# A graph network's first table built in groups of six tiles, and the table of the other ends moved into the first edge stage

## The chip, the cores and the metric

The kernel runs on one core of one Trainium2 chip. A core has five engines that run their own instruction queues: TensorE (PE in the profile; PEld is its weight load), VectorE (DVE), ScalarE (ACT), GpSimd (POOL) and SyncE (SP), which here only issues DMA transfers. They wait for each other through semaphores. The metric is the device time of the whole program in microseconds (us); lower is better. Besides plain runs there is one profiled execution, from which the profile comes.

## The reference

Two layers of a graph network run on 6250 nodes with 128 features and 106250 edges, which come sorted by their target node `dst`. In what the change touches, only the first layer counts:

```python
h = jnp.maximum(_layernorm(x, axis=-1), 0.0)
...
xl = x @ Wl + bl        # here x is h
xr = x @ Wr + br
e = edge_attr @ We
m = xl[src] + xr[dst] + e
m = jax.nn.leaky_relu(m, NEG_SLOPE)
logits = m @ att
...                     # softmax over the edges of one dst
out = jax.ops.segment_sum(xl[src] * alpha[:, None], dst, num_segments=n)
```

The second layer forms a message from `x[src]` and `x[dst]` of every edge, sums the messages over `dst`, and mixes the sum with the node's own features.

## The kernel before

**Tables.** The nodes are 49 tiles of 128. Two tables are made from the normalised features and written to device memory: `xl_d`, whose rows (128 values and one more, h·Wl·att scaled) are gathered by `src`, and `xr_d`, the table of the other ends, whose rows are read in windows, since `dst` is sorted. The first stage ("table stage", lines 218 to 291) makes both. It goes through seven groups of seven tiles. For a group, VectorE takes the statistics of every tile (L237, L238), ScalarE and VectorE make the scale and shift (L240 to L242). For each tile, ScalarE then makes `h` (L248), TensorE transposes it into PSUM (`tp`, L251), VectorE or ScalarE by turns copies it out into `h_sb`, where it stands by feature and is kept (L253), TensorE multiplies it with both weights side by side, 257 columns (`mm`, L255), VectorE adds the bias of the first part and stores it as `tl` (L256), and ScalarE copies the second part as `tr` (L257). One write for `tl` and one for `tr` leave per group through SP's queue (L258, L259). `h`, `tp`, `mm`, `tl` and `tr` have two buffers each. After the first group, the list of source nodes, loaded as rows, is turned into columns by eight transposes (`columns`, L203 to L210, called at L263); the gathers take their indices from these. The stage also looks at the order of the edges and makes a flag (L270 to L291), which every engine reads in order to branch: `general()` is a way for all inputs, `fast()` the one that is run here.

**First edge stage.** `fast()` prepares small tables (L780 to L843: edge weights and indices as columns, masks) and then runs the loop of L1020 over 104 steps of 1024 edges. Step `s` loads its window of `xr_d` into `W`, and the row `dlb` of local target numbers (`load`, L851); GpSimd issues eight indirect gathers of 128 rows of `xl_d` each into a tile `gl` (`gather`, L195 to L198), of which there are ten buffers; VectorE compares `dlb` with the partition's number (`one_hot_t`, L863); TensorE multiplies this with `W` (`expand`, L867), which spreads the window's rows to the edges; VectorE adds the gathered rows (L1033), and logits follow. Seven steps later (`LAG`, L893) the gathered rows of step `u = s - 7` are weighted with the softmax's factors (L1049), summed by a matmul (L1063) and stored; then their `gl` buffer is free.

**Later stages.** The node stage (L1100 to L1171) makes two tables for the second layer, and the second edge stage (L1286) gathers from one of them in the same manner, with 832 more gathers. It is not touched by the change.

**What sets the order.** In the two edge loops the order of each engine's instructions is that of the program text. In the table stage and in the preparing part of `fast()` a scheduler orders each engine's instructions; every engine then works its own queue strictly in order, and one waiting instruction holds up all behind it. SP's queue is in order too, waits included. A DMA that is issued from SP or ScalarE also waits for an earlier one whose semaphore it uses again.

Of the kernel before, what the change touches and what calls it, by code (L numbers as in the profile page):

```python
# [27 lines left out]
TG = 7  # L28
NG = NT // TG
# [7 lines left out]
WIN = 126  # L37
PACE = 60
SLACK = 96
TN = 4  # L40
NGR = NT // TN
CH = TN * P
WL = D + 1
# [5 lines left out]
def kernel(  # L49
# [39 lines left out]
    x_sb = state.tile([P, NT, D], F32, name="x_sb")  # L89
    h_sb = state.tile([P, NT, D], F32, name="h_sb")  # L90
# [3 lines left out]
    for g in range(NG):  # L94
        n = TG if g < NG - 1 else TG - 1
        nc.sync.dma_start(
            x_sb[:, g * TG : g * TG + n, :],
            x[g * TG * P : (g * TG + n) * P, :].rearrange("(t p) f -> p t f", p=P),
        )
# [3 lines left out]
    ident = consts.tile([P, P], F32, name="ident")  # L103
# [96 lines left out]
    def node_rows(table, g, n=TG):  # L200
        return table[g * TG * P : (g * TG + n) * P].rearrange("(t p) ... -> p t ...", p=P)
# [13 lines left out]
    xl_d = dram.tile([NP, WL], F32, name="xl_d")  # L215
    xr_d = dram.tile([NP + P, D], F32, name="xr_d")
    flag = consts.tile([1, 1], I32, name="flag")
    with tc.tile_pool(name="pre", bufs=2) as pp, tc.tile_pool(name="pre1", bufs=1) as p1, tc.tile_pool(
# [14 lines left out]
        for g in range(NG):  # L233
            mv = pp.tile([P, TG, 2], F32, name="mv")
            for j in range(TG):
                st = pp.tile([P, 6], F32, name="st")
                V.bn_stats(st, x_sb[:, g * TG + j, :])  # L237
                V.bn_aggr(mv[:, j, :], st)  # L238
            rstd = pp.tile([P, 2, TG], F32, name="rstd0")
            S.activation(rstd[:, 0, :], mv[:, :, 1], AF.Sqrt, bias=eps)  # L240
            V.reciprocal(rstd[:, 0, :], rstd[:, 0, :])
            V.scalar_tensor_tensor(rstd[:, 1, :], mv[:, :, 0], -1.0, rstd[:, 0, :],  # L242
                                   op0=ALU.mult, op1=ALU.mult)
            tl = pp.tile([P, TG, WL], F32, name="tl")
            tr = pp.tile([P, TG, D], F32, name="tr")
            for j in range(TG):
                h = pp.tile([P, D], F32, name="h")
                S.activation(h, x_sb[:, g * TG + j, :], AF.Relu, bias=rstd[:, 1, j : j + 1],  # L248
                             scale=rstd[:, 0, j : j + 1])
                tp = ps_p.tile([P, P], F32, name="tp")  # L250
                T.transpose(tp, h, ident)  # L251
                hT = h_sb[:, g * TG + j, :]
                (S.copy if j % 2 else V.tensor_copy)(hT, tp)  # L253
                mm = ps_p.tile([P, 2 * D + 1], F32, name="mm")
                T.matmul(mm, hT, w0c, start=True, stop=True)  # L255
                V.tensor_tensor(tl[:, j, :], mm[:, :WL], b0c, ALU.add)  # L256
                S.copy(tr[:, j, :], mm[:, WL:])  # L257
            nc.sync.dma_start(node_rows(xl_d, g), tl)  # L258
# [482 lines left out]
    def fast():  # L741
# [43 lines left out]
        with tc.tile_pool(name="col1", bufs=1) as p1, tc.tile_pool(name="rows", bufs=2) as rp, tc.tile_pool(  # L785
            name="ps_p", bufs=2, space=PSUM
        ) as ps_p:
# [6 lines left out]
            nc.sync.dma_start(dl_d, dl_b)  # L794

# [589 lines left out]
```

## Time and profile before

| | us |
|---|---|
| median of 3 runs | 3032.93 (3027.8 to 3052.9) |
| profiled execution, its own time | 2414.23 |
| its span, first to last instruction | 2412.4 |
| POOL busy in the span | 1699.7 (70%) |
| DVE busy | 1637.3 (68%) |
| PE busy | 1375.8 (57%) |
| ACT busy | 1276.6 (53%) |

The profiled execution is 619 us shorter than the median of the plain runs; the profile says nothing of where the plain runs spend these. In the span, the table stage takes the first 65 us, gathers from `xl_d` run from 71.6 us to about 1147 us, the node stage lies about 1150 to 1235 us, and the second edge stage fills nearly all of the rest.

A line of the costliest groups has the source line, the engine, the operation, what it writes and reads, and a count; then busy time and mean ns of one, and the idle time of the engine just before it with what ended that. A line of an answer in order of time has start and duration in us, engine, line and operation, and in brackets the idle time before it. A line of waits has who waited for whom, the sum in us, how often, and the longest one. The chain that ended last follows the work back from the last instruction to whatever released it.

### The profile page before, as it was taken

The numbers are of one execution on the slowest core, as the hardware profiler recorded it, in microseconds if no ns is written. First come the engines' busy times: TensorE is split into PE (matmuls) and PEld (weight loads), VectorE is DVE, ScalarE is ACT, GpSimd is POOL, SyncE is SP. The second block draws the span as 40 slices with busy tenths as digits, with TensorE's granted clock in tenths as the row PEclk, the third lists the DMA queues.
The fourth block names the chain that finished last, engine by engine and source line by source line (L and its number), as shares of the span: only waits on it lengthen the run. The fifth ranks groups of instructions, "written<-read, shape, count | busy, mean of one in ns | idle before, by whom it ended". The sixth has DMA issues, their size and how long they took to land.

```text
span 2412.4 us, 30614 instructions
## 1 busy us (share of the span) xinstructions
PE 1375.8 (57%) x7692; PEld 1270.8 (53%) x7692; DVE 1637.3 (68%) x3597; ACT 1276.6 (53%) x4267; POOL 1699.7 (70%) x1703
## 2 busy tenths in 40 slices
PE   6446555556566556565484555555655655555553
PEld 3345555555555455565464555555555654555553
DVE  6666677677677667767445567677767768768765
ACT  5223343334344334344456676676676677667663
POOL 1677777777777777777057777777777777777770
PEclk9667887787878777777687677778777777777876
DMA  6743455443443433443142333343333333333331
GB/s 166 211 114 92 111 151 137 98 100 92 101 100 92 98 96 92 100 100 80 32 132 79 90 94 99 85 107 97 83 107 97 85 108 103 83 101 102 85 96 30
DMA packets 217496, 242.90 MB, mean 101 GB/s; under 512 B 41373, under 2 KB 158077, under 8 KB 217309
## 3 DMA queue, kind: packets, MB, share of 16 engines
q0 software_dynamic: 53792, 110.57, 19.7%
q1 hardware_dynamic: 160657, 130.00, 18.5%
q8 instruction: 64, 1.05, 0.2%
q14 instruction: 123, 1.01, 0.1%
q10 hardware_dynamic: 2860, 0.27, 0.1%
HBM read 197.43 MB, written 43.25 MB: 100 GB/s over the span
## 4 chain that ended last, share of the span: by engine, by line
POOL 44%; issue 18%; DMA 14%; DVE 13%; PE 7%; ACT 3%; SPq 0%; DVEq 0%; another core or an unknown queue 0%; ACTq 0%; POOLq 0%
POOL gl L196 44%; DMA gl<-xl_d,src_c 7%; DMA gl<-a_d,src_c 5%; DVE y L1314 2%; DVE m_ps L1033 2%; PE agg_ps L1063 2%; DVE y L1298 1%; DVE oh L1309 1%; PE agg_ps L1329 1%; DVE y L1316 1%; PE mm L255 1%; PE mm L1156 1%; ACT sq L1303 1%; DVE oh L1040 1%; DVE oht L863 1%
## 5 line engine op out<-in xcount | busy, mean ns | idle before, releaser
L196 POOL DMA_INDIRECT gl<-xl_d,src_c x832 | 820.9, 987 | 308.8 <-issue 229.8
L196 POOL DMA_INDIRECT gl<-a_d,src_c x832 | 845.2, 1016 | 260.7 <-issue 234.3
L1329 PE MATMUL agg_ps<-glw,oh 128*128 128x129 f32 x1664 | 363.9, 403 | 485.7 <-ACT glw L1320 439.7
L1329 PEld LDWEIGHTS agg_ps<-glw,oh 128*128 128x128 f32 x1664 | 336.3, 298 | 505.8 <-ACT glw L1320 505.8
L1063 PE MATMUL agg_ps<-glw,oh 128*128 128x130 f32 x1664 | 345.0, 389 | 386.3 <-DVE glw L1043 206.8
L1063 PEld LDWEIGHTS agg_ps<-glw,oh 128*128 128x128 f32 x1664 | 320.7, 288 | 404.1 <-ACT glw L1049 404.1
L1034 ACT ACTIVATE m_ps<-m_ps 128x1024 f32<-128x1024 f32 x104 | 104.8, 1008 | 573.6 <-DVE m_ps L1033 429.3
L1303 ACT ACTIVATE sq<-y 128x128 f32<-128x128 f32 x832 | 257.1, 309 | 275.8 <-DVE y L1298 252.4
L1033 DVE TENSOR_TENSOR m_ps<-m_ps,gl 128x1024 f32<-128x1024 f32 x104 | 128.1, 1232 | 299.9 <-DMA gl<-xl_d,src_c 273.7
L867 PE MATMUL m_ps<-W,oht 128*128 128x128 f32 x1664 | 259.8, 320 | 36.2 <-DVE oht L863 22.8
L867 PEld LDWEIGHTS m_ps<-W,oht 128*128 128x128 f32 x1664 | 243.8, 233 | 45.2 <-issue 22.3
L1320 ACT ACTIVATE glw<-y,ew_c 128x128 f32<-128x128 f32 x832 | 254.4, 389 | 3.4
L1049 ACT ACTIVATE glw<-gl,exm 128x128 f32<-128x128 f32 x832 | 254.3, 394 | 0.0
L1298 DVE TENSOR_TENSOR y<-y_ps,gl 128x1024 f32<-128x1024 f32 x104 | 126.8, 1220 | 187.8 <-DMA gl<-a_d,src_c 146.7
L867 PE MATMUL y_ps<-W,oht 128*128 128x128 f32 x1664 | 230.4, 298 | 13.2 <-DVE oht L863 9.0
L867 PEld LDWEIGHTS y_ps<-W,oht 128*128 128x128 f32 x1664 | 226.7, 218 | 13.8 <-issue 13.8
L1314 DVE SCALAR_TENSOR_TENSOR y<-y,rs,mg_r 128x128 f32<-128x128 f32 x832 | 227.3, 344 | 0.0
L863 DVE TENSOR_SCALAR oht<-dlb,iota_p 126x1024 f32<-126x1024 bf16 x208 | 159.3, 766 | 15.1 <-DMA dlb<-dl_d 15.0
L1303 ACT ACTIVATION_READ_ACCUMULATOR sq<-y 128x1 f32 x832 | 155.0, 186 | 0.0
L1051 DVE TENSOR_TENSOR m_ps<-m_ps,att 128x1024 f32<-128x1024 f32 x104 | 131.3, 1263 | 4.8 <-ACT m_ps L1034 4.6
L1317 ACT ACTIVATE y<-y 128x1024 f32<-128x1024 f32 x104 | 109.9, 1057 | 41.1 <-DVE y L1316 41.0
L1316 DVE TENSOR_TENSOR y<-y,mb_r 128x1024 f32<-128x1024 f32 x104 | 127.7, 1228 | 3.6
(251 smaller groups left out, 1610.7 us busy)
## 6 DMA issues: line engine op xcount, KB each, us to landing
dlb<-dl_d SPq DMA_DIRECT2D x208, 256.0 KB
gl<-xl_d,src_c POOLq DMA_INDIRECT x832
gl<-a_d,src_c POOLq DMA_INDIRECT x832
res<-agg SPq DMA_DIRECT2D x104, 64.0 KB
res<-agg SPq DMA_DIRECT2D x104, 63.5 KB
W<-xr_d SPq DMA_DIRECT2D x104, 63.0 KB
W<-b_d SPq DMA_DIRECT2D x104, 63.0 KB
res<-zt SPq DMA_DIRECT2D x20, 325.0 KB
```

Source lines behind the costliest of these rows:

```text
L196: GP.indirect_dma_start(out=dest, out_offset=None, in_=table, in_offset=bass.IndirectOffsetOnAxis(ap=idx, axis=0))
L863: V.tensor_scalar(oht[:WIN, :], dlb[:WIN, :], iota_p[:WIN, :], None, op0=ALU.is_equal)
L867: T.matmul(ps[:, j, :], oht[:, j * P : (j + 1) * P], w, start=True, stop=True)
L1033: V.tensor_tensor(ps, ps, gl[:, :, :D], ALU.add)
L1049: S.activation(glw[:, j, :D], glu[:, j, :D], AF.Copy, scale=exm[b][:, q, j, 1:2])
L1063: T.matmul(aggs[u], oh[:, j, :], glw[:, j, :], start=(j == 0), stop=(j == ST - 1))
L1298: V.tensor_tensor(y, pss.pop(s), gl, ALU.add)
L1303: S.activation(sq, y[:, j, :], AF.Square, accum_out=rs[:, j : j + 1])
L1314: V.scalar_tensor_tensor(yu[:, j, :], yu[:, j, :], ru[:, j : j + 1], mg_r, op0=ALU.mult, op1=ALU.mult)
L1316: V.tensor_tensor(yu, yu, over_tiles(mb_r, ST), ALU.add)
L1320: S.activation(glw[:, j, :D], yu[:, j, :], AF.Copy, scale=ew_c[:, u, j : j + 1])
L1329: T.matmul(aggs[u], oh[:, j, :], glw[:, j, :], start=(j == 0), stop=(j == ST - 1))
```

## The change

The table stage now goes through groups of six tiles (the last has one). Three tiles share a PSUM tile: three transposes are followed by one copy of 384 columns, always on ScalarE, and three matmuls of 129 columns by one addition of the bias on VectorE. The weight tile holds only the first table's columns. The source list is turned into columns at the fourth group rather than the first, and `x` is loaded in eight groups of six tiles. The table of the other ends is no longer made here: in `fast()`, behind the write of the local target numbers, 13 groups of four tiles are multiplied straight from the kept `h_sb` with `Wr`, copied out of PSUM by ScalarE into one of two `tr` buffers, and written to `xr_d` on SP's queue, all ahead of the first load of a window.

```diff
+PG = 6
+PB = 3
...
-    for g in range(NG):
-        n = TG if g < NG - 1 else TG - 1
+    for g in range(NT // PG):
         nc.sync.dma_start(
-            x_sb[:, g * TG : g * TG + n, :],
-            x[g * TG * P : (g * TG + n) * P, :].rearrange("(t p) f -> p t f", p=P),
+            x_sb[:, g * PG : (g + 1) * PG, :],
+            x[g * PG * P : (g + 1) * PG * P, :].rearrange("(t p) f -> p t f", p=P),
         )
...
-        w0c = p1.tile([P, 2 * D + 1], F32, name="w0c")
+        w0c = p1.tile([P, WL], F32, name="w0c")
         b0c = p1.tile([P, WL], F32, name="b0c")
-        V.tensor_copy(w0c[:, WL:], w0[:, D:])
...
-        for g in range(NG):
-            mv = pp.tile([P, TG, 2], F32, name="mv")
-            for j in range(TG):
+        for t0 in range(0, NT, PG):
+            n = min(PG, NT - t0)
+            mv = pp.tile([P, PG, 2], F32, name="mv")
+            for j in range(n):
...
-            tl = pp.tile([P, TG, WL], F32, name="tl")
-            tr = pp.tile([P, TG, D], F32, name="tr")
-            for j in range(TG):
-                h = pp.tile([P, D], F32, name="h")
-                S.activation(h, x_sb[:, g * TG + j, :], AF.Relu, bias=rstd[:, 1, j : j + 1],
-                             scale=rstd[:, 0, j : j + 1])
-                tp = ps_p.tile([P, P], F32, name="tp")
-                T.transpose(tp, h, ident)
-                hT = h_sb[:, g * TG + j, :]
-                (S.copy if j % 2 else V.tensor_copy)(hT, tp)
-                mm = ps_p.tile([P, 2 * D + 1], F32, name="mm")
-                T.matmul(mm, hT, w0c, start=True, stop=True)
-                V.tensor_tensor(tl[:, j, :], mm[:, :WL], b0c, ALU.add)
-                S.copy(tr[:, j, :], mm[:, WL:])
-            nc.sync.dma_start(node_rows(xl_d, g), tl)
-            nc.sync.dma_start(node_rows(xr_d, g), tr)
-            if g == 0:
+            tl = pp.tile([P, PG, WL], F32, name="tl")
+            for q in range(0, n, PB):
+                k = min(PB, n - q)
+                tp = ps_p.tile([P, PB, P], F32, name="tp")
+                for j in range(q, q + k):
+                    h = pp.tile([P, D], F32, name="h")
+                    S.activation(h, x_sb[:, t0 + j, :], AF.Relu, bias=rstd[:, 1, j : j + 1],
+                                 scale=rstd[:, 0, j : j + 1])
+                    T.transpose(tp[:, j - q, :], h, ident)
+                S.copy(h_sb[:, t0 + q : t0 + q + k, :], tp[:, :k, :])
+                mm = ps_p.tile([P, PB, WL], F32, name="mm")
+                for j in range(k):
+                    T.matmul(mm[:, j, :], h_sb[:, t0 + q + j, :], w0c, start=True, stop=True)
+                V.tensor_tensor(tl[:, q : q + k, :], mm[:, :k, :],
+                                b0c[:, None, :].to_broadcast([P, k, WL]), ALU.add)
+            nc.sync.dma_start(xl_d[t0 * P : (t0 + n) * P].rearrange("(t p) f -> p t f", p=P), tl[:, :n, :])
+            if t0 == 3 * PG:
                 sr = p1.tile([NS, SE], F32, name="sr")
                 V.tensor_copy(sr, src_r)
                 columns(ps_k, src_c, sr, "ctp")
...
             nc.sync.dma_start(dl_d, dl_b)
+
+            for t0 in range(0, NT, TN):
+                n = min(TN, NT - t0)
+                rp_ = ps_x.tile([P, TN, D], F32, name="xr_ps")
+                for j in range(n):
+                    T.matmul(rp_[:, j, :], h_sb[:, t0 + j, :], w0[:, D:], start=True, stop=True)
+                tr = xp.tile([P, TN, D], F32, name="tr")
+                S.copy(tr[:, :n, :], rp_[:, :n, :])
+                nc.sync.dma_start(xr_d[t0 * P : (t0 + n) * P].rearrange("(t p) f -> p t f", p=P), tr[:, :n, :])
 
             for w in Ws:
```

More of the change, by code (lines that the diff above doesn't have):

```diff
@@ L232 @@
             V.tensor_scalar(o[:, D : D + 1], o[:, D : D + 1], 0.2, None, op0=ALU.mult)
-        for g in range(NG):
-            mv = pp.tile([P, TG, 2], F32, name="mv")
-            for j in range(TG):
+        for t0 in range(0, NT, PG):
+            n = min(PG, NT - t0)
+            mv = pp.tile([P, PG, 2], F32, name="mv")
+            for j in range(n):
                 st = pp.tile([P, 6], F32, name="st")
-                V.bn_stats(st, x_sb[:, g * TG + j, :])
+                V.bn_stats(st, x_sb[:, t0 + j, :])
@@ L238 @@
                 V.bn_aggr(mv[:, j, :], st)
[L239 to L242, printed above, removed]
+            rstd = pp.tile([P, 2, PG], F32, name="rstd0")
+            S.activation(rstd[:, 0, :n], mv[:, :n, 1], AF.Sqrt, bias=eps)
+            V.reciprocal(rstd[:, 0, :n], rstd[:, 0, :n])
@@ L243 @@
+            V.scalar_tensor_tensor(rstd[:, 1, :n], mv[:, :n, 0], -1.0, rstd[:, 0, :n],
                                    op0=ALU.mult, op1=ALU.mult)
-            tl = pp.tile([P, TG, WL], F32, name="tl")
-            tr = pp.tile([P, TG, D], F32, name="tr")
-            for j in range(TG):
-                h = pp.tile([P, D], F32, name="h")
-                S.activation(h, x_sb[:, g * TG + j, :], AF.Relu, bias=rstd[:, 1, j : j + 1],
-                             scale=rstd[:, 0, j : j + 1])
-                tp = ps_p.tile([P, P], F32, name="tp")
-                T.transpose(tp, h, ident)
-                hT = h_sb[:, g * TG + j, :]
-                (S.copy if j % 2 else V.tensor_copy)(hT, tp)
-                mm = ps_p.tile([P, 2 * D + 1], F32, name="mm")
-                T.matmul(mm, hT, w0c, start=True, stop=True)
-                V.tensor_tensor(tl[:, j, :], mm[:, :WL], b0c, ALU.add)
-                S.copy(tr[:, j, :], mm[:, WL:])
@@ L785, in fast @@
         with tc.tile_pool(name="col1", bufs=1) as p1, tc.tile_pool(name="rows", bufs=2) as rp, tc.tile_pool(
-            name="ps_p", bufs=2, space=PSUM
-        ) as ps_p:
+            name="xr", bufs=2
+        ) as xp, tc.tile_pool(name="ps_p", bufs=2, space=PSUM) as ps_p, tc.tile_pool(
+            name="ps_x", bufs=2, space=PSUM
+        ) as ps_x:
             base_f = p1.tile([NS, 1], F32, name="base_f")
```

## The prediction

> **What bounds the kernel now.** I read the chain of work that ended last, then the costliest groups, then GpSimd's waits, then the first 72 us in order of time. The page first:
>
> ```profile
> span 2412.4 us, 30614 instructions
> ...
> POOL 44%; issue 18%; DMA 14%; DVE 13%; PE 7%; ACT 3%; SPq 0%; DVEq 0%; another core or an unknown queue 0%; ACTq 0%; POOLq 0%
> ...
> L196 POOL DMA_INDIRECT gl<-xl_d,src_c x832 | 820.9, 987 | 308.8 <-issue 229.8
> ```
>
> GpSimd's gathers carry the chain. In the first edge stage there are 832, each 0.987 us plus idle before it; without one long wait that is (820.9 + 308.8 - 55.6)/832 = 1.291 us, so 10.33 us for a step of eight. GpSimd's waits up to 1260 us, where the second edge stage begins:
>
> ```profile
> POOL gl L196 <- issue: 230.4, 756, 0.3
> POOL x_sb L1134 <- PE ctr L1126: 80.4, 12, 63.9
> POOL gl L196 <- DMA W<-in_L_gnn_br_dram: 55.6, 1, 55.6
> POOL gl L196 <- DMA gl<-xl_d,src_c: 10.1, 33, 0.3
> ```
>
> No gather waits over 0.3 us for a buffer or a consumer; the one long wait, 55.6 us, is that of the first gather for the first table. So **the time of the first gather is worth its full length**: all that follows hangs on it. The end of the table stage in order of time:
>
> ```profile
> 65.06 0.29 DVE L256 TENSOR_TENSOR tl<-mm,b0c 128x129 f32<-128x129 f32 x1 [0.25 <-PE mm L255]
> 65.39 0.36 SPq L258 DMA_DIRECT2D xl_d<-tl  x1
> ...
> 69.59 0.60 DVE L780 MEMSET zt<- 128x650 f32 x1 [4.23 <-issue]
> ...
> 71.57 1.26 POOL L196 DMA_INDIRECT gl<-xl_d,src_c  x1 [55.55 <-DMA W<-in_L_gnn_br_dram]
> ```
>
> The last eviction ends at 65.35, its write of seven tiles lands 5.23 us after its issue (the chain's piece, 65.39 to 70.62), and the gather starts 0.95 later. The releaser named on the gather is only the latest event; the chain itself goes through the write. The stage's groups, up to 71 us:
>
> ```profile
> L255 PE MATMUL mm<-w0c,h_sb 128*128 128x257 f32 x98 | 33.5, 449 | 1.3 <-DVE h_sb L253 0.7 <-DVE mv L238 0.3
> L248 ACT ACTIVATE h<-x_sb,rstd 128x128 f32<-128x128 f32 x49 | 23.5, 495 | 4.5 <-PE tp L251 2.3 <-DMA x_sb<-in_x_dram 2.1
> ```
>
> From 30.0 to 65.4 TensorE is busy 33.3 of 35.4 us, ScalarE 30.1, VectorE 28.4 (busy time by stretch): TensorE is nearly full, ScalarE 85%. Before that everything stood from about 24 to 29.2 us for the source indices, whose load took 11.46 us.
>
> **What the Trainium skill says.** "PSUM — Partial Sum Buffer", The four PSUM rules: one matmul output stays in one 2 KiB bank. Three tiles of 129 words are 1548 B and fit, four would not; no run shows a limit here. "ScalarE: Activation LUTs", What ACT_TABLE_LOAD costs: 186 ns + 0.833 ns per element, 93 ns more for each pointer operand; h would be 479 ns, the trace has 495, it agrees. "DMA: Bandwidth & Descriptors", Anatomy of one DMA: about 2 us of a transfer are fixed; a gather's landing here is 2.44 us, which agrees. "Runtime: NRT & Kernel Launch", Instruction fetch mechanics: a taken branch can force a fetch; VectorE's 4.23 us above agree.
>
> **The change, part by part.**
> *Removed from the table stage.* The matmul has 129 columns in place of 257. Its two passes run at 0.33 us each in close bursts (six in 1.98); the 128-column m_ps matmul runs 0.128 a pass (sixteen in 2.05), so 2 x 0.33 falls to 2 x 0.13 = 0.26 us: 0.4 us a tile off TensorE. Gone are 49 copies tr (0.262 us, ScalarE) and seven xr_d writes.
> *Batched.* Three transposes, one ScalarE copy of 384: between the 128 copy (0.263) and the 512 one (0.586) that is 0.48 us. One VectorE add of 387: between 0.291 (129) and 1.232 (1024) that is 0.56 us.
> *What is left after the stall.* The order of the changed program has 15 tiles transposed before the source columns (before: 9), with 12 multiplied (before: 6). The index load is the same and queues behind the same 3.2 MB of x, so I keep 29.2 us and start at 30.0; that the columns moved to the fourth group gains six tiles of cover, but no earlier index. Then ScalarE has 33 h x 0.495 = 16.3, 11.3 copies x 0.48 = 5.4, two column copies 1.8, five roots 1.5: 25.1 us. TensorE: 34 transposes x 0.28 + 37 x 0.26 to 0.32 + 1.8 = 21 to 23. VectorE: 22 tiles x 0.44 statistics + 13 adds x 0.56 + about 7 for flags and reciprocals = 24. **ScalarE becomes the longest, with the others close.** At the old stretch of 35.4/30.1 = 1.18 it takes 29.6, unstretched 25.1; I take 27.4. The last three tiles' matmul and add: 1.0. The last write is now one tile, behind one of six: between 2.4 (a gather) and 5.2, I take 3.8, plus 0.95. First gather at 30.0 + 27.4 + 1.0 + 3.8 + 0.95 = 63.2 against 71.57: -8.4. Ends: 59.5 (-12.1) and 66.8 (-4.8). The new x groups (eight loads in place of seven) and the weight copy L227 (0.23) come before the stall and cost nothing as long as 29.2 stands.
> *Moved into the edge stage.* 49 matmuls (2 x 0.128 = 0.26: 12.5 us TensorE), 13 copies of 512 (0.586: 7.6 us ScalarE), 13 writes on SP. TensorE and ScalarE stand there anyway: up to 94.8 and 100.2 us they do little but column transposes. On SP the writes stand ahead of the loads of W, dlb and edge weights of step 0, and W reads xr_d, so it waits for all 13. The index and weight loads lie between them. On ScalarE the later copies hold up its queued column loads and the column copies; VectorE waits for the end-of-row loads. tr has two buffers: a pair costs a copy 0.59 + issue 0.41 + landing 3.8 = 4.8, and 6.5 pairs take 31 us. The last eviction is at 58.4 by the sum above, the branch takes the 4.23 us that it took before: 62.6. Then come 1.5 to begin, the 31, and 8.3 as before from the first dlb load (90.64) to the first add of gathered rows (98.94): the first add at 103.4, which is 40 us after the first gather (before: 27). **The cover:** ten gl buffers. Step 10's gathers start 103 us after the first; they need gl of step 0, freed in round 7, that is 7 x 5.8 (98.94 to 104.73) + 4 after the first add. So the add may come 58.7 us after the first gather; 18 us of slack remain, and the cost is nothing. Without that cover every microsecond of the 40 would be on the path.
> *Contention.* xr_d's 3.2 MB now run beside the first gathers, where 71 to 160 us already moves 182 GB/s. I take 1 us, from 0 to 4.
> *Sum:* -8.4 + 1 = -7.4 us on the profiled time of 2414.23 (span 2412.4 + 1.8 around it). The three timed runs' median is 3032.93, 619 us above it; the profile doesn't show where these lie. If they are spread evenly everything counts 1.256 times (-9.3), if they lie elsewhere once. I take -8: **3025**. With the ends, (-12.1) x 1.256 = -15 and -0.8.
>
> **The rivals.** Three runs of the kernel before differ by 25 us (3027.8 to 3052.9), so about 1%, 30 us, is what a measurement can tell from no change.
> *The stage doesn't shorten.* h keeps two buffers: a copy ends, three matmuls take 0.9 with their wait, the next transpose 0.27, then 0.2, one h 0.5, the copy 0.48, about 2.6 in all with waits: 0.87 us a tile, against 0.86 before (35.4/41). For: TensorE works in order, its transposes stand behind the matmuls, and ScalarE then idles between an h and the next though it has the most to do. Against: the order that was drawn up varies along the stage, in places four transposes run ahead of a matmul. With 34 tiles x 0.87 = 29.6, 1.8 for the column copies, 1.0, 3.8 and 0.95 the first gather is at 67.1, and 2 us later where VectorE's flag work (7 us) falls into that chain: -2 to -4, less 1 of contention; I take 3031.
> *Slower: the table of other ends comes too late.* Mechanism: two tr buffers, 13 writes in a row ahead of W. It decides from a landing of 6.6 us ((58.7 + 0.6 - 9.8)/6.5 - 1.0). Speaking for it: src_r took 11.46 under load. At that landing the pairs take 6.5 x 12.46 = 81, the first add is 32 us past the slack, net +24: 3057; at 14 us the pairs take 97.5, net +40: 3073; at 9 us they take 65, net +8: 3041. I take 3060. Against: the writes are small (256 KB), xl_d's of 452 KB landed in 5.23.
> *The hidden 619 us lie in the front.* If the unprofiled start is much longer than 71 us, a shorter one gains more: a gain of 40 in place of 8, 2993. Nothing in the profile speaks for it, nothing excludes it.
>
> **How the numbers follow.** Forecast 0.60 (3025); stage doesn't shorten 0.15 (3031); too late 0.10 (3060); front longer 0.15 (2993). The first two are within 1%; of the third half lies over +1% (landings past 12.5 us), half below. Faster by over 1% 0.15, within 1% 0.80, slower 0.05. The range takes the ends of the sum, 3033 - 15 and 3033 - 0.8, and half the runs' spread (12.5) on either side: 3005 to 3045. It leaves out the last rival (0.15) and the worse half of the third (0.05), and holds the rest.
>
> **What would show it.** Right: the first gather between 59 and 67 us, the gathers still 1.29 us apart, no wait over a microsecond on gl after it, span about 2405. ScalarE, not TensorE, fullest from 30 us on. Batching wrong: first gather later than 68. Lateness: a wait of GpSimd for ScalarE's glw near the eleventh step. Source stall wrong: the cast of the indices not near 29 us. The whole is wrong if the unprofiled time moves by more than 30 us while the span doesn't.

## The result and the profile after

| | us |
|---|---|
| before, median of 20 runs | 3033.97 (3022.09 to 3052.9) |
| after, median of 20 runs | 3065.35 (3033.55 to 3080.96) |
| after / before | 1.0085, 95% interval 1.0059 to 1.011 |
| after, the profiled execution's own time | 3073.72 (span 3071.9) |

The changed kernel is slower by 0.85%, 31 us between the medians. 3025 was forecast, with 3005 to 3045 as the range.

The kernel before runs at one of two levels, near 2414 us or near 3030 us (2990 us in one set), and keeps to one for a whole set of runs made beside each other on one chip; its first profile is of the short level, its timed runs above are of the long one.

The page of the changed kernel, to be set against the first fence of the prediction:

```profile
span 3071.9 us, 30732 instructions
...
DVE 25%; another core or an unknown queue 24%; ACT 22%; PE 13%; issue 11%; DMA 3%; POOL 1%; DVEq 0%; SPq 0%; ACTq 0%; POOLq 0%
...
L197 POOL DMA_INDIRECT gl<-xl_d,src_c x832 | 817.1, 982 | 660.8 <-ACT glw L1061 345.2
L197 POOL DMA_INDIRECT gl<-a_d,src_c x832 | 817.2, 982 | 541.9 <-DVE y L1310 286.6
```

GpSimd's gathers carried 44% of the chain before and carry 1% now; they wait for ScalarE's glw and VectorE's y. These are the gathered rows weighted with the softmax's factors in the first edge stage, and what the second one makes of its gathered rows; a gl buffer is free only when they are made. Most of this is not the change, though. A second profile of the kernel before, `before_again`, is of the long level (3034.98 us). GpSimd's waits there, and then those of the changed kernel from 60 to 300 us (who waited for whom, sum in us, times, longest):

```profile
POOL gl L196 <- issue: 467.3, 1485, 8.1
POOL gl L196 <- ACT glw L1049: 325.2, 43, 48.7
POOL gl L196 <- DVE y L1298: 279.3, 54, 12.0
```

```profile
POOL gl L197 <- ACT glw L1061: 73.1, 1, 73.1
POOL gl L197 <- DMA W<-in_L_gnn_We_dram: 51.9, 1, 51.9
POOL gl L197 <- issue: 43.2, 114, 8.8
```

The two waits of before are 604.5 us in all. The first profile had neither, and its span was 620.8 us shorter: this is where the "hidden 619 us" lie, spread over both edge stages. What the change adds is in the one long wait near the eleventh step: 73.1 in place of 48.7 us.

The front of three profiled executions, from their answers in order of time (the 81st gather is the first one that needs a freed gl buffer):

| us | before, short level | before, long level | after, long level |
|---|---|---|---|
| first gather | 71.57 | 71.24 | 68.79 |
| first add of gathered rows | 98.94 | 145.36 | 199.57 |
| 81st gather | 176.96 | 222.62 | 245.65 |

Against the long level, the first gather comes 2.5 us earlier and the 81st 23.0 us later. The two executions are 38.7 us apart (3034.98 and 3073.72, the latter 8 us above its kernel's median): 23.0 us lie up to the 81st gather, 15.7 behind it. From the 81st gather to the end of the span four executions of set 1 below took 2801 to 2816 us and this one 2826, so the 15.7 us can't be told from the scatter of single executions.

**The preparing part, after.** ScalarE and then VectorE in order of time (start, duration, engine, line; in brackets the idle time before and what ended it; `remote` is a releaser that the profile doesn't name, `issue` none that it shows):

```profile
98.08 0.90 ACT L211 COPY dl_c<-ctp 128x416 f32<-128x416 f32 x1 [4.30 <-PE ctp L209]
...
118.69 0.90 ACT L211 COPY dl_c<-ctp 128x416 f32<-128x416 f32 x1 [19.53 <-issue]
129.89 0.90 ACT L211 COPY fst_c<-ctp 128x416 f32<-128x416 f32 x1 [10.30 <-issue]
141.09 0.90 ACT L211 COPY fst_c<-ctp 128x416 f32<-128x416 f32 x1 [10.30 <-issue]
141.78 1.12 ACT L805 COPY tr<-xr_ps 128x512 f32<-128x512 f32 x2
182.41 0.90 ACT L211 COPY ew_c<-ctp 128x416 f32<-128x416 f32 x1 [39.51 <-remote]
```

```profile
194.95 0.75 DVE L875 TENSOR_SCALAR oht<-dlb,iota_p 126x1024 f32<-126x1024 bf16 x1 [46.22 <-DMA W<-xr_d]
...
199.57 1.23 DVE L1045 TENSOR_TENSOR m_ps<-m_ps,gl 128x1024 f32<-128x1024 f32 x1 [1.99 <-PE m_ps L879]
```

VectorE's first one-hot tile and first addition in the kernel before at the long level:

```profile
106.58 0.98 DVE L863 TENSOR_SCALAR oht<-dlb,iota_p 126x1024 f32<-126x1024 bf16 x1 [12.78 <-issue]
...
145.36 1.23 DVE L1033 TENSOR_TENSOR m_ps<-m_ps,gl 128x1024 f32<-128x1024 f32 x1 [30.94 <-remote]
```

In the changed kernel, GpSimd issues the 80 gathers of the ten gl buffers from 68.8 to 172 us, one behind the other. Up to 98 us the others work; then copies that take a microsecond stand 10 to 40 us apart. The work picks up about 10 us after the last of the 80 gathers (171.61), and only then is the table of other ends finished.

The same is seen in the loop of the kernel before at the long level. TensorE, VectorE and some of GpSimd's gathers:

```profile
614.77 0.20 PE L926 MATMUL tx<-ident,crow 1*32 1x1 f32 x2
...
622.80 0.94 POOL L196 DMA_INDIRECT gl<-xl_d,src_c  x1 [0.30 <-issue]
624.05 0.94 POOL L196 DMA_INDIRECT gl<-xl_d,src_c  x1 [0.30 <-issue]
627.53 0.15 DVE L929 COPY cc<-tx 32x2 f32<-32x2 f32 x1 [7.39 <-remote]
```

The copy at 627.53 needs the two transposes that ended at 614.97. It comes 12.6 us later, 2.5 us after the end of the last gather of a series, though VectorE had stood for 7.39 us. A lower granted TensorE clock (its mean is 0.688 here, 0.764 in the first profile) can't be the reason: the transposes were long done.

**The table stage, after.** Where the prediction counted on 8.4 us, there are 2.5 to 2.8. TensorE alone in stretches of 6 us (stretch, length, busy time and count, granted clock, DMA share, GB/s), before at the long level and then after:

```profile
36.00:42.00 6.00, 5.92 (x26) 1.00 0.63 160
48.00:54.00 6.00, 5.99 (x25) 1.00 0.57 150
54.00:60.00 6.00, 5.54 (x26) 1.00 0.62 161
```

```profile
36.00:42.00 6.00, 4.87 (x28) 0.92 0.44 125
48.00:54.00 6.00, 5.26 (x22) 0.50 0.18 53
54.00:60.00 6.00, 5.26 (x21) 0.50 0.27 79
```

From about 41 us on the batched stage runs at half the granted TensorE clock. The additions to tl, three tiles each, are then 2.82 us apart:

```profile
57.03 0.56 DVE L258 TENSOR_TENSOR tl<-mm,b0c 128x387 f32<-128x387 f32 x1 [1.99 <-PE mm L257]
...
59.85 0.56 DVE L258 TENSOR_TENSOR tl<-mm,b0c 128x387 f32<-128x387 f32 x1 [2.26 <-PE mm L257]
```

In an execution with the same stage whose clock was still 1.00 (`tr13`, below) they are 1.99 us apart:

```profile
51.00 0.56 DVE L258 TENSOR_TENSOR tl<-mm,b0c 128x387 f32<-128x387 f32 x1 [1.17 <-PE mm L257]
52.99 0.56 DVE L258 TENSOR_TENSOR tl<-mm,b0c 128x387 f32<-128x387 f32 x1 [1.43 <-PE mm L257]
```

### The profile page after: what moved, and what is told of

Its sections match the earlier page's. It is cut to its first block, busy times and chain, and to the rows that moved or that the text cites. A ratio compares the mean times of both kernels' runs of the same rounds, so it can differ in the third digit from the quotient of the medians.

```text
span 3071.9 us, 30732 instructions
## 1 busy us (share of the span) xinstructions
PE 1490.3 (49%) x7790; PEld 1338.4 (44%) x7790; DVE 1618.3 (53%) x3540; ACT 1282.7 (42%) x4229; POOL 1667.6 (54%) x1703
## 4 chain that ended last, share of the span: by engine, by line
DVE 25%; another core or an unknown queue 24%; ACT 22%; PE 13%; issue 11%; DMA 3%; POOL 1%; DVEq 0%; SPq 0%; ACTq 0%; POOLq 0%
ACT sq L1315 9%; PE agg_ps L1341 6%; ACT glw L1332 6%; DVE m_ps L1045 3%; DVE lr L1065 3%; ACT y L1329 3%; DVE m_ps L1063 3%; DVE oh L1052 3%; DVE y L1310 2%; DVE y L1326 2%; ACT glw L1061 2%; POOL gl L197 1%; PE agg_ps L1075 1%; DVE oh L1321 1%
## 5 line engine op out<-in xcount | busy, mean ns | idle before, releaser
L197 POOL DMA_INDIRECT gl<-a_d,src_c x832 | 817.2, 982 | 541.9 <-DVE y L1310 286.6
L1341 PE MATMUL agg_ps<-glw,oh 128*128 128x129 f32 x1664 | 433.6, 435 | 663.2 <-ACT glw L1332 491.3
L1075 PE MATMUL agg_ps<-glw,oh 128*128 128x130 f32 x1664 | 315.7, 364 | 532.3 <-ACT glw L1061 320.0
L879 PE MATMUL m_ps<-W,oht 128*128 128x128 f32 x1664 | 277.9, 322 | 160.9 <-issue 134.9
L879 PEld LDWEIGHTS m_ps<-W,oht 128*128 128x128 f32 x1664 | 250.8, 231 | 182.9 <-issue 152.8
L879 PE MATMUL y_ps<-W,oht 128*128 128x128 f32 x1664 | 267.8, 328 | 32.8 <-issue 23.8
L879 PEld LDWEIGHTS y_ps<-W,oht 128*128 128x128 f32 x1664 | 265.0, 249 | 33.1 <-issue 33.1
L1065 DVE TENSOR_REDUCE lr<-m_ps 128x8 f32<-128x1024 f32 x104 | 127.4, 1225 | 3.6
```

Of the source, the lines that this page charges most:

```text
L197: GP.indirect_dma_start(out=dest, out_offset=None, in_=table, in_offset=bass.IndirectOffsetOnAxis(ap=idx, axis=0))
L879: T.matmul(ps[:, j, :], oht[:, j * P : (j + 1) * P], w, start=True, stop=True)
L1065: V.tensor_reduce(lr, ps, AX.X, ALU.add)
L1075: T.matmul(aggs[u], oh[:, j, :], glw[:, j, :], start=(j == 0), stop=(j == ST - 1))
L1341: T.matmul(aggs[u], oh[:, j, :], glw[:, j, :], start=(j == 0), stop=(j == ST - 1))
```

## The experiments

The theory after the result: at the long level the other engines fall behind while gathers follow each other closely; the change puts more work (13 groups of matmul, copy and write, and W behind all of them) into the stretch where this happens, and so the ten gl buffers, which the prediction took for cover, are what holds the work up. Rivals: the batched stage itself costs the time; the writes ahead of W do, whatever the gathers; time is a plain sum of gathers and other work, which no placing of gathers changes. Runs came in six sets, each with its own runs of the kernel before: medians 3031.45, 2989.76, 2414.87, 2413.74, 3031.75 and 3037.2 us. Ratios are against the set's own; intervals are 95%.

### Before once more (set 1)

No edit.

> The kernel before, looked at once more, because its first profiled execution took 2414 us and its timed runs 3033. If the front loss of the changed kernel is new, the first add of gathered rows comes about 27 us after the first gather here too, and no wait of GpSimd for ScalarE's glw near the eleventh step exceeds 1 us. If an execution of some 3033 us always has the other engines standing while gathers run one behind the other, its span is near 3030 us, the first add comes 80 to 110 us after the first gather, and GpSimd has a wait of 20 to 50 us for glw near the eleventh step, shorter than the 73 us of the changed kernel.

3034.98 us; first add 74.1 us after the first gather, the second at 182.43, longest wait for glw 48.7 us. The second theory of the expectation holds, with the first add a little earlier than it said: the hold-up is there without the change, and smaller.

### Each part alone (set 1)

The stage batched, the table of other ends kept in it, as an edit of the changed kernel (the second part is in fast()):

```diff
+                mx = ps_p.tile([P, PB, D], F32, name="mx0")
+                for j in range(k):
+                    T.matmul(mx[:, j, :], h_sb[:, t0 + q + j, :], w0[:, D:], start=True, stop=True)
+                S.copy(tr[:, q : q + k, :], mx[:, :k, :])
...
-            for t0 in range(0, NT, TN):
...
```

> Only the table stage is batched (six tiles to a group, three to an eviction); the table of other ends is still made there, by matmuls and copies of three tiles. Theory that the move costs the time: ratio 0.99 to 1.002, first gather between 66 and 73 us, the wait near the eleventh step no longer than in the kernel before. Theory that the batching itself costs it: ratio 1.005 to 1.015.

The stage of the kernel before without its second product, and the 13 groups of the changed kernel in fast(), as an edit of the kernel before:

```diff
-        w0c = p1.tile([P, 2 * D + 1], F32, name="w0c")
+        w0c = p1.tile([P, WL], F32, name="w0c")
...
-                S.copy(tr[:, j, :], mm[:, WL:])
...
+            for t0 in range(0, NT, TN):
...
```

> The table stage is as before (seven tiles to a group, one to an eviction) but without the table of other ends, which is made in the first edge stage as in the changed kernel. Theory that the move costs the time: ratio 1.006 to 1.014, a wait of GpSimd for glw near the eleventh step of 60 to 80 us. Theory that the batching costs it: ratio 0.995 to 1.002.

stage_only: 3033.11 us, 1.0015 (0.9997 to 1.0032). move_only: 3048.03 us, 1.0069 (1.0046 to 1.0093). The two add up to 1.0084, and the change as a whole is 1.0085 in the set of the result: **the move costs the time**, the batching little or nothing. Two expectations failed in the profiles. stage_only's first gather came at 78.69, later than said (66 to 73), and cost nothing that can be told: its 81st gather came at 221.05, against 222.62 in the kernel before. At the long level, then, the first gather is not worth its length; the wait near the eleventh step takes it up. And move_only's longest wait was 49.3 us, not 60 to 80, in an execution of 3039.75 us, well below that kernel's median; the verdict rests on its 16 runs.

### Gathers held until the preparation is done (set 1)

```diff
+        src_g = fs.tile([P, NS, ST], I32, name="src_g")
...
             for s in range(2):
                 one_hot_t(*wins[s])
+            V.tensor_copy(src_g, src_c)
...
-                        gather(gl[:, j, :], xl_d, src_c[:, s, j : j + 1])
+                        gather(gl[:, j, :], xl_d, src_g[:, s, j : j + 1])
```

> The changed kernel with its gathers held back: they read a copy of the source indices that VectorE makes only behind the first two one-hot tiles of the edge stage. Theory that the gathers running ahead slow the other engines in the preparation: preparation that took 126 us from the first gather to the first add takes 35 to 50 us when no gather runs, so the first gather comes at 100 to 115 us and the time is 3010 to 3045. Theory that the writes of the table or the preparation are slow by themselves: the first gather comes at 180 to 200 us and the time is 3100 to 3130.

3060.55 us, 1.0109 (1.0076 to 1.0143). The preparation came as the theory said, first gather at 112.71: VectorE makes the first one-hot tile 40.0 us after it begins fast() (69.01 to 109.03), where this took 126.5 us (68.42 to 194.95) with gathers beside it. The time was missed (3010 to 3045), since the hold-up moved. The additions of gathered rows:

```profile
124.33 1.23 DVE L1047 TENSOR_TENSOR m_ps<-m_ps,gl 128x1024 f32<-128x1024 f32 x1 [11.90 <-DMA gl<-xl_d,src_g]
137.11 1.23 DVE L1047 TENSOR_TENSOR m_ps<-m_ps,gl 128x1024 f32<-128x1024 f32 x1 [6.85 <-issue]
148.84 1.23 DVE L1047 TENSOR_TENSOR m_ps<-m_ps,gl 128x1024 f32<-128x1024 f32 x1 [5.86 <-remote]
192.97 1.23 DVE L1047 TENSOR_TENSOR m_ps<-m_ps,gl 128x1024 f32<-128x1024 f32 x1 [38.09 <-remote]
```

The additions stand 12 us apart here, against 5.8 us in the changed kernel once its loop runs, and from 154.88 on, 42 us after the first gather, VectorE stands for 38.09 us: the others stop again, now in the loop. The 81st gather comes at 248.06 (changed kernel: 245.65). Gathers beside the preparation slow it threefold; that is shown. Moving the whole series behind it gains nothing.

### More buffers, no chain, a shorter series, fewer gl (set 2)

Thirteen `tr` buffers and four PSUM tiles:

```diff
-            name="xr", bufs=2
+            name="xr", bufs=13
...
-            name="ps_x", bufs=2, space=PSUM
+            name="ps_x", bufs=4, space=PSUM
```

> The changed kernel with thirteen tr buffers in place of two and four PSUM tiles for them in place of two, so that no copy of the table of other ends waits for a write to land. Theory that the two buffers stretch the chain into the time in which the gathers hold up everything: the thirteen groups are through TensorE and ScalarE by 90 us, the first add of gathered rows comes at 140 to 165 us in place of 199.6, the wait near the eleventh step falls from 73 to 40 to 55 us, and the time is 3025 to 3045. Theory that thirteen writes ahead of W cost the time whatever the buffers: first add at 190 to 205 us, time 3060 to 3070.

Without the moved work (this leaves out the product h·Wr, and the table holds the input features):

```diff
-            for t0 in range(0, NT, TN):
...
+            nc.sync.dma_start(xr_d[: NT * P].rearrange("(t p) f -> p t f", p=P), x_sb)
```

> The changed kernel without the work on the table of other ends: no matmuls, no copies, and one write that fills the table with the input features in place of thirteen with the product, so the output is not the reference's. Theory that this work is the loss: ratio 0.990 to 1.002 and first add at 130 to 150 us. Theory that the batched stage or the later order is the loss: ratio 1.006 to 1.012.

Steps 3 to 11 gather only after the add of three steps before:

```diff
+        srcs = {s: fs.tile([P, ST], I32, name=f"src_{s}") for s in range(3, 12)}
...
-                        gather(gl[:, j, :], xl_d, src_c[:, s, j : j + 1])
+                        gather(gl[:, j, :], xl_d, srcs[s][:, j : j + 1] if s in srcs else src_c[:, s, j : j + 1])
...
                     V.tensor_tensor(ps, ps, gl[:, :, :D], ALU.add)
+                    if s + 3 in srcs:
+                        V.tensor_copy(srcs[s + 3], src_c[:, s + 3, :])
```

> The changed kernel with the gathers of steps 3 to 11 each held until the add of three steps before (their indices are copied by VectorE right after that add), so that at the start at most 24 gathers run ahead in place of 80; afterwards all is as before. Theory that the long run of gathers is what holds the other engines up: first add at 105 to 135 us, no wait of GpSimd for glw above 15 us near the eleventh step, time 3000 to 3040. Theory that time is simply the sum of gathers and the other engines' work, whatever the length of the runs: the waits of GpSimd only move to the adds, time 3055 to 3075.

Nine gl buffers:

```diff
-        gp = g0.enter_context(tc.tile_pool(name="e0g", bufs=10))
+        gp = g0.enter_context(tc.tile_pool(name="e0g", bufs=9))
```

> The changed kernel with nine gl buffers in place of ten in the first edge stage: at the start 72 gathers run ahead in place of 80, and in the steady part GpSimd is at most two steps ahead of the consumer. Theory of long runs: first add 8 to 12 us earlier than 199.6, and the steady steps no longer, time 3035 to 3065. Theory of the sum: less overlap is left, time 3070 to 3150.

| | us | ratio | first gather | first add after it | longest wait for glw |
|---|---|---|---|---|---|
| tr13 | 2998.44 | 1.0029 (1.0007 to 1.005) | 61.26 | 36.7 | 31.6 |
| nochain | 2993.75 | 1.0015 (1.0002 to 1.0029) | 65.83 | 41.2 | 35.5 |
| paced3 | 2985.42 | 0.9987 (0.9974 to 1.0001) | 69.89 | 60.0 | 9.3 |
| gl9 | 3002.51 | 1.0043 (1.0018 to 1.0068) | 61.52 | 111.9 | 64.3 |

The times cannot be set beside those of set 1, and the changed kernel was not in this set, so the ratios carry the reading, if they carry over from one set to another. The numbers of the front are of single executions; that of tr13 is 20 us under its kernel's median. With thirteen buffers (and four PSUM tiles) the copies are through by 79 us, before the others fall behind, the first add is at 97.95, and the ratio is 1.0029 in place of 1.0085: waiting for the two tr buffers carries much of the move's cost. The front went further than the theory said (first add 140 to 165, wait 40 to 55), the ratio did not. Without the work it is 1.0015, inside the interval of tr13; the first add, at 107.04, came earlier than said (130 to 150). In tr13 and nochain the 81st gather comes at 199.13 and 205.73, earlier than in the kernel before of set 1 (222.62), and still neither is faster than its own kernel before; that one wasn't profiled in this set, so how much of the front reaches the time isn't shown. Pacing, which keeps the chain and its two buffers but lets 24 gathers run ahead in place of 80, does at least as well as leaving the work out. GpSimd's waits in paced3 show that it does what it says:

```profile
POOL gl L197 <- ACT glw L1064: 259.1, 41, 9.3
...
POOL gl L197 <- DVE src L1048: 28.8, 1, 28.8
```

It waits 28.8 us once for the first add (at 129.84; 105 to 135 was expected), and never over 9.3 us for glw. With nine buffers the first add comes at 173.37, 26.2 us earlier than in the changed kernel (8 to 12 were expected); 7.3 of these are an earlier first gather. The ratio is 1.0043; without the changed kernel beside it the size of the gain is open.

### The change and a mended version at both levels (sets 3, 4 and 5)

The changed kernel again:

> The changed kernel itself, as the yardstick beside the next three on the same chip. Expected: ratio 1.006 to 1.011 as measured before, first add of gathered rows 110 to 135 us after the first gather, the 81st gather 170 to 180 us after the first, a wait of 65 to 80 us for glw near the eleventh step.

> The changed kernel once more, as the yardstick on whichever chip this is. Where the kernel before takes some 2414 us: ratio 0.997 to 1.000 as measured there. Where it takes 2990 to 3035 us: ratio 1.006 to 1.011, the 81st gather 170 to 180 us after the first, a wait of 65 to 80 us for glw near the eleventh step.

The mended version joins tr13's and paced3's edits and gives `h` six buffers:

```diff
-                    h = pp.tile([P, D], F32, name="h")
+                    h = pp.tile([P, D], F32, name="h", bufs=6)
```

> The changed kernel with three edits at once: six h buffers in the table stage, thirteen tr buffers and four PSUM tiles, and the gathers of steps 3 to 11 held until the add of three steps before. Theory that the two h buffers set the pace of the batched stage: the last additions to tl come 0.7 us a tile or less apart in place of 0.94, first gather 4 to 9 us earlier than the changed kernel's. Theory that the long run of gathers holds up the moved work: first add 35 to 45 us after the first gather, the 81st gather 105 to 130 us after it, ratio 0.982 to 0.995. If TensorE's order and not the buffers sets the stage, first gather within 2 us of the changed kernel's and the ratio 0.985 to 0.999.

> Six h buffers, thirteen tr buffers and gathers held to three steps ahead at the start. Where the kernel before takes some 2414 us: ratio 0.999 to 1.002 as measured there. Where it takes 2990 to 3035 us and the theory holds that the long run of gathers holds up the moved work: first add 35 to 45 us after the first gather, 81st gather 105 to 135 us after it, ratio 0.982 to 0.997. If the moved work isn't what costs the time there: ratio 1.005 or more.

> Six h buffers, thirteen tr buffers, gathers held to three steps ahead at the start. Where the kernel before takes 2990 to 3035 us: theory that the long run of gathers holds up the moved work: first add 35 to 45 us after the first gather, 81st gather 105 to 135 us after it, ratio 0.982 to 0.997; if the moved work isn't what costs the time: 1.005 or more. Where it takes some 2414 us: ratio 0.999 to 1.002.

| | level | us | ratio |
|---|---|---|---|
| after_again | short | 2411.52 | 0.9985 (0.9974 to 0.9996) |
| after_third | short | 2411.88 | 0.9989 (0.9975 to 1.0003) |
| combo | short | 2414.68 | 1.0005 (0.9992 to 1.0018) |
| combo_second | short | 2416.11 | 1.0009 (0.9997 to 1.0021) |
| combo_third | long | 3015.66 | 0.9953 (0.9934 to 0.9972) |

after_again's numbers for the front were expected for the long level and do not apply; the chip was of the short one. There the change costs nothing: it is 3.4 and 1.9 us faster between the medians, and only the first of the two intervals stays below 1. So the 1.0085 of the long level was measured once, in the result. GpSimd's waits in after_third:

```profile
POOL gl L197 <- issue: 475.5, 1560, 0.3
POOL x_sb L1146 <- PE ctr L1138: 85.6, 12, 65.8
POOL gl L197 <- ACT tr L805: 50.5, 1, 50.5
```

After the first gather (67.3) none waits over 0.3 us for a buffer or a consumer. The first add comes 47.8 us after it, inside the prediction's 58.7. The mended version is 0.47% faster than the kernel before at the long level and not to be told from it at the short one. Its first add there came 47.7 us after the first gather (35 to 45 were expected) and its 81st gather 129.6 us after it, as expected.

### A pause behind every gather (sets 3 to 6)

```diff
     def gather(dest, table, idx):
...
+        GP.memset(pad, 0.0)
```

`pad` has 64 elements a partition in the first three runs and 256 in the last two; nothing reads it.

> The changed kernel with a small memset on GpSimd (64 elements a partition, of a tile that nothing reads) behind every gather, in both edge stages, so that gathers stand 0.2 to 0.6 us further apart. Theory that the other engines fall behind because gathers follow each other too closely, and that a short pause clears it: the waits of GpSimd for glw and y fall from some 630 us to below 150 and the time is 2750 to 2980. Theory of the sum, where a pause only moves: 3040 to 3090. Theory that the other engines need something other than GpSimd's pauses: 1664 pauses are added to the time, 3350 to 3700.

> A small memset on GpSimd behind every gather. Where the kernel before takes some 2414 us: ratio 1.022 to 1.028 as measured there. Where it takes 2990 to 3035 us: theory that gathers following each other closely hold up the other engines and that a short pause clears it: ratio 0.82 to 0.96, the waits for glw and y together below 150 us in place of some 630. Theory of the sum, where a pause only moves: 1.00 to 1.02. Theory that the pauses are added to the time: 1.03 to 1.10.

> As the earlier two with 64 elements, in the hope of a chip on which the kernel before takes 2990 to 3035 us. There: theory that gathers following each other closely hold up the other engines and that a short pause clears it: ratio 0.82 to 0.96, the waits for glw and y together below 150 us in place of some 630. Theory of the sum, where a pause only moves: 1.00 to 1.02. Theory that the pauses are added to the time: 1.03 to 1.10. Where the kernel before takes some 2414 us: 1.022 to 1.028.

> As the one with 64 elements, with a memset of 256 elements: about three times the added pause, 0.5 to 1.2 us. Where the short pause already clears it, this one is slower than that by 0.3 to 0.6 us a gather, 500 to 1000 us. Under the theory of the sum 3040 to 3300. If 64 elements were too short, this is the faster of the two.

> The memset of 256 elements behind every gather, which on the chip where the kernel before takes some 2414 us widened the gathers' distance by 0.20 us and cost 336 us. Where the kernel before takes 2990 to 3035 us: theory that a pause of this size clears the hold-up: below 2950 us. Theory that the time is gathers plus the other engines' work and that the pauses count as time for the others: 3000 to 3100. Theory that the pauses are simply added: 3330 to 3400. On a chip where the kernel before takes some 2414 us: ratio 1.137 to 1.142 again.

| | level | us | ratio |
|---|---|---|---|
| space64 | short | 2474.55 | 1.0252 (1.0222 to 1.0282) |
| space64_second | short | 2475.96 | 1.0264 (1.0238 to 1.029) |
| space64_third | long | 3030.82 | 1.0006 (0.9984 to 1.0027) |
| space256 | short | 2750.44 | 1.1396 (1.1371 to 1.1422) |
| space256_second | long | 2750.31 | 0.9083 (0.9047 to 0.9118) |

What was expected of the first space64 and of space256 was meant for the long level. The short memset hardly paused anything. It runs in a gap that is there anyway, so that gathers start 1.28 us apart in place of 1.25. At the long level its 1.0006 lies where the theory of the sum put it, and the waits for glw and y are 536.7 us, not below 150: so short a pause does not clear the hold-up. GpSimd in space64_third:

```profile
601.41 0.95 POOL L199 DMA_INDIRECT gl<-xl_d,src_c  x1 [0.16 <-issue]
602.36 0.17 POOL L202 MEMSET pad<- 128x64 f32 x1
602.69 0.95 POOL L199 DMA_INDIRECT gl<-xl_d,src_c  x1 [0.16 <-issue]
```

The longer one puts the gathers 1.44 us apart. With it the kernel takes 2750 us at both levels: the difference of 620 us is gone. In order of time, and then the longest sums of GpSimd's waits, space256_second:

```profile
604.10 0.95 POOL L199 DMA_INDIRECT gl<-xl_d,src_c  x1 [0.17 <-issue]
605.04 0.33 POOL L202 MEMSET pad<- 128x256 f32 x1
605.54 0.95 POOL L199 DMA_INDIRECT gl<-xl_d,src_c  x1 [0.17 <-issue]
```

```profile
POOL gl L199 <- issue: 281.9, 1659, 1.9
POOL x_sb L1149 <- PE ctr L1141: 84.0, 12, 64.8
POOL gl L199 <- DMA W<-in_L_gnn_We_dram: 52.3, 1, 52.3
```

No wait for glw or y is left. 3000 to 3100 (pauses are time for the others) and 3330 to 3400 (pauses are added) are both refuted: at the long level the closely spaced gathers **cause** the others' standing, and a memset behind each, which puts 0.19 us more between them, ends it. Whether the distance does it or the memset itself isn't separated. It is 9.2% faster than the kernel before there, and 14% slower at the short level, where the pauses are only added. An added distance between 0.03 and 0.19 us, and a pause in the kernel before, were not tried.

## Why the prediction was wrong

**The first add "40 us after the first gather", and so "18 us of slack remain, and the cost is nothing".** This step failed. The arithmetic is nearly right where the engines run freely: 47.8 us at the short level, no wait. At the long level the first add comes 130.8 us after the first gather, and GpSimd waits 73.1 us, 24.4 more than in the kernel before. The step took the ten gl buffers as cover, and asked only how long they last. It did not ask what 80 gathers without a stop do to the work under them: hold_after shows that preparation takes 40 us without them and 126 with them. By the ratios of set 2, tr13 takes most of the loss away by finishing the work before the others fall behind, and paced3 all of it by shortening the series.

**Contention: "I take 1 us, from 0 to 4."** The term that was meant for this was mis-sized, and looked in the wrong place, at bytes per second. The net of contention and lost cover is about 23 us at the 81st gather. Slower transfers are not the reason: by the pages, the packets of GpSimd's queue took 15.1% of the long span of before_again, 458 us, and 19.7% of the short span, 475 us.

**"The profile doesn't show where these lie" (the 619 us).** They were taken for neutral, spread or elsewhere. 604 of them were waits that the profile at hand did not have, so "no gather waits over 0.3 us for a buffer or a consumer", on which everything stood, did not hold in the runs that were to be predicted. The rival that put them into the front saw only a gain in it. A second profile of the kernel before, of the long level, would have told.

**"So the time of the first gather is worth its full length."** False at the long level, where stage_only's was 7 us later for nothing. At the short level the 81st gather moved with the first (172.63 after a first at 67.3, 176.96 after 71.57), but the medians differ by 1.9 us only, with 1 inside the interval: that the time follows in full isn't shown.

**The first gather at 63.2 us, from 59.5 to 66.8.** The sum fits executions whose granted clock stayed at 1.00 until 54 us: tr13, gl9, space64, space64_second and space256 had the first gather at 61.26 to 63.9. In the other eight executions with this stage, the changed kernel's own three among them (68.79, 71.37 and 67.3), the clock fell to 0.50 before that; three tiles then take 2.82 us, against 1.99. The sum had no term for this; its own sign for the batching being wrong, a first gather later than 68, came true. "ScalarE becomes the longest" held in tr13 (ScalarE busy 20.78 us, TensorE 18.56, from 30 to 54 us) and failed in the changed kernel's profile (from 30 to 63 us, TensorE 27.93 and ScalarE 20.96). The rival "the stage doesn't shorten" gave 67.1 or some more, right in size, but for another reason: it had 0.87 us a tile from the two h buffers, and tr13, with the same two, takes 0.66. With six h buffers and the clock at 1.00 (combo_third, near 50 us) three tiles take 1.72 us, so the two buffers cost 0.27 us for three tiles, some 3 us over 34 tiles (an estimate); the clock costs 0.83 for three.

**The slower rival.** It named the place (table of other ends too late), the sign in the trace (a wait for glw near the eleventh step) and 3060 us, 5 from the measured 3065. Its mechanism was wrong: it decided at a landing of 6.6 us, and on the chain that ended last the first write landed in 5.29 and later ones in 2.3. It got 0.10, since the trace spoke against slow writes, and slow writes were the only way to lateness that was considered.

**What stays open.** Why a set is of one level or the other: each of the six sets ran on a chip of its own, and no chip was seen at both levels. And what the gathers block: signals between engines seem to come late (12.6 us for a copy on VectorE), while TensorE, ScalarE, VectorE and SP all stand, but instructions that reach their engines late would look the same, and no run tells the two apart. What kind of pause is needed, or whether the memset does it in another way than by time, wasn't tried.

## What to carry to other kernels

Before a profile is used, its own time is to be set beside the timed runs; where they differ by a fifth, the waits that bound the timed runs may be missing from it, and a second profile comes first. Slack that consists of one engine running far ahead is slack only if that running doesn't slow the work under it: finish such work before it starts, or limit how far ahead it may go. A shortened stage can run at a lower granted TensorE clock than the one before it, as 8 of 13 executions did here, so it is priced at both clocks.

## What the runs showed of the hardware

- Closely spaced indirect gathers (1.25 us from start to start) can hold up all other engines; at 1.44 us, with a memset between them, this was gone: 2750.31 us where the kernel before takes 3037.2, and 2750.44 where it takes 2414.87.
- How far into a series the others stop differs, even from rest. VectorE's last instruction before it stood for 30 us or more began 30 us after the first gather in the changed kernel, 41 in hold_after and 58 in tr13. In the loop of the kernel before, in a series from 604.54, VectorE's last before 7.39 us of standing began after 14 us.
- In the table stage the granted TensorE clock was 1.00 or 0.50, with means between only where a stretch holds both. "TensorE: Matmul & The Clock Gate" of the Trainium skill, Part 1, tells of half rate after an idle window of about 3.4 us and full rate after a busy one. The kernel before agrees: its clock falls in its stall before 30 us and is back at 1.00 from 36 us. In the changed kernel a gap of 3.80 us before 30.41 left it at 1.00, and in move_only one of 7.22 us before 30.80 did; then it fell with TensorE at work, at about 41 us in one execution of the changed kernel (busy 4.87 of the 6 us from 36 to 42), 48 in another and 44 in move_only. In stage_only it stood at 1.00 from 36 to 66 us with TensorE busy only 21.91 of these 30 us. So the page's two rates are seen; its rule for the fall is seen in the kernel before and not in these executions.
